# Two recurrent layers in fp32: the second layer's xn transposed in 32x32 blocks by VectorE and carried to its partitions by DMAs, the first layer's additions made by accumulating DMAs

## The chip, the cores and the metric

The kernel runs on one core of one Trainium2 chip. The metric is the device time of one launch in microseconds (us), taken as the median of several runs. Engines are named as in the profile: PE is TensorE's matrix products, PEld its weight loads, DVE is VectorE, ACT is ScalarE, POOL is GpSimd, SP is SyncE, whose queue issues most of the DMAs. The core has an on-chip memory of 128 partitions (SBUF) and a smaller accumulator memory (PSUM), into which TensorE writes its products in banks of 128x512 fp32.

## The reference

The input x is (4, 512, 256) in fp32: four batches of 512 rows. Two layers follow each other. Cut to what matters:

```python
x = L0_attn_x                                   # (B, S, D) = (4, 512, 256)
xn = _layernorm(x)                              # no gain, no offset
s = xn + rmsnorm(((xn @ W_in.T) * g) @ W_out.T) * norm_w     # first layer's mixer, g = sum(C_r*B_r - C_i*B_i)
x = x + s * silu(ffn0(xn))
xn = _layernorm(x)
h = layernorm(xn) * gamma + beta                # second layer's mixer: causal attention
s = softmax(mask(q(h) @ k(h).T / 16)) @ v(h) @ o_proj + xn
x = x + s * silu(ffn1(xn))
# ffn(xn) = fwht(silu(xn @ W1.T) * (xn @ W3.T)) @ W2.T, hidden width 1024, fwht a fixed 1024x1024 matrix
```

The state of the first layer's recurrence starts at zero and is used for one step, so that its mixer is linear up to the RMS norm, as written above. Each layer thus needs xn twice: by rows (for the residual and the gate) and transposed (features on the partitions), because TensorE contracts over partitions.

## The kernel before, in words

**Numbers.** TensorE multiplies fp32 by parts: each operand is held as a rounded part `hi` and the rest `lo`, and a product is three products, hi·hi, hi·lo and lo·hi (`mm3`). `split` (L59 to L62) makes the parts: ScalarE copies `hi` (L61), VectorE subtracts to get `lo` (L62). All matrix products and transposes are issued by one helper line, L70; in the profile they are told apart by their tiles.

**First layer.** It goes by batches 0 to 3. `ffn` (L470) runs over eight chunks of the hidden width. A chunk has two up products (tiles `f_1gu` and so on, twelve matmuls of 128x512 into the banks `gu`, of which there are three), the silu (ScalarE, L531), the product of both halves (VectorE, L533, tile `h`), its split, and the down products of the chunk before (`dn`, 12 matmuls of 128x256). Each chunk has two slots in which other work is issued (`Beside`): the batch's own mixer, the gate of the batch before, the layernorm of the next batch (`norm`, L434) and the preparation of weights. `mixer` (L721) multiplies xn by one folded matrix into the tile `osb`, norms it (L734 to L738: `ssr` holds the mean squares, POOL takes the power -1/2, four VectorE operations scale `osb`), and adds it into the rows of xn (L741, one operation of 128x1024). `gate` (L697) takes the silu of the down products (ScalarE, L704), multiplies it by xn (VectorE, L710, two operations of 128x512, tile `g`) and adds it into x (L712, two of 128x512). A scheduler that works on a simulated timeline orders the instructions of each engine in this layer; `after(...)` adds an order that it has to keep.

**Second layer.** From the last gate of the first layer on, TensorE's order is written out by hand (`line["fixed"] = True`, L1083, `in_line`). For each batch `ffn_s` (L568) goes through four quarters of the hidden width. A quarter has seven products of blocks (`A11`·`B11`, `S1`·`T1`, ... , each six matmuls of 128x256) and between them eight places; `places[q][n]` lists the steps that are issued at place n of quarter q. An integer in the list is a group of six down products of the quarter before (`behind`). The weights of a quarter, 14 blocks of 128x256 in two tiles `sw`, come by two DMAs of 896 KB (L351) from the DRAM tiles `s` that the first layer has written (`prep_s`). The other steps are the attention of the same batch (`v`, `sc`, `soft`, `pt`, `pv`), the gate of the batch before (`gate_half`, then `later_gates`), and what the next batch needs:

- `norm(1, b)` has three steps: the layernorm (L264 to L280: statistics, POOL's power L278, four VectorE operations L280 that write the rows of xn); the second norm's scale `mr` (`second_norm`, L256); and a transpose of `mr`, which goes through a DRAM tile and comes back as `mrb`, one value per row on all partitions.
- `Attention.xt_half(k)` (L751) has TensorE transpose half k of xn into a PSUM bank, four transposes of 128x128.
- `Attention.xt` (L755) makes from the two banks the blocks that the next batch's products need: the sums t1 to t4, the splits `tb11` and `tb2x`, and the products with `mrb` (`fs`); ScalarE copies one half bank (`b12`) first, since an operation of VectorE here takes one operand from PSUM.
- `scaled` (L776) makes the attention's input `xg` from `fs`, `split_sums` (L785) splits t1 to t4, and `tq` (L788) is the first product that reads `xg`.

For batch 0 these steps stand in the slots of the last batch of the first layer. For batches 1 to 3 the transposes and `xt` stand in places 1 and 2 of quarter 2 of the batch before. Pools of tiles set when memory comes free: `t4` has 10 buffers of 4 KB a partition, `t2` 6, `hid` 14, `xn` 3; PSUM has three banks `ms` for transposes and attention, three `gu` and two `dn`. SyncE's queue issues in program order the loads of x and weights, the writes of `s`, the loads of `sw`, `rows` and `mrb` (L452, L454) and the stores of the output (L1054, L1070); an issue whose data is not ready holds up those behind it.

Of the kernel before, what the change touches and what calls it, by code (L numbers as in the profile page):

```python
# [11 lines left out]
F32 = mybir.dt.float32  # L12
# [9 lines left out]
P = 128  # L22
D = 256
# [12 lines left out]
def kernel(ctx: ExitStack, tc: tile.TileContext, a: dict, out: bass.AP):  # L36
# [263 lines left out]
    ALLS = slice(0, S)  # L300
    ALLD = slice(0, D)

    xns, xTs, mrs = {}, {}, {}

    def xt_pair(name):

# [70 lines left out]
    def norm_first():  # L377
# [53 lines left out]
        first["norm"] = hi_, lo_  # L431
        yield

    def norm(layer, b):  # L434
        xn = act.tile([P, NT, D], F32, tag="xn", name=f"xn{layer}_{b}", bufs=3)
        xns[layer, b] = xn
        with after(first["gate"] if b > 1 - layer else None):
            first["scaled"], mv, r = layernorm(f"ln{layer}_{b}", xs[b], xn)
        yield
        if layer:  # L440


            mr = act.tile([P, NT], F32, tag="mr", name=f"mr{b}", bufs=2)
            second_norm(mr, mv, r)
            yield
            o = psum(f"mrp{b}", [NT, P], **DN[b == 0])
            transpose(o, mr, ident)
            rows = act.tile([NT, P], F32, tag="rows", name=f"rows{b}", bufs=1)
            with after(first["table"] if b else None):
                nc.scalar.copy(rows, o)  # L450
            there = dram.tile([NT, P], F32, tag="rows", name=f"there{b}")
            nc.sync.dma_start(there, rows)  # L452
            mrb = t4(f"mrb{b}", [P, S])
            nc.sync.dma_start(  # L454
                mrb, there.rearrange("t p -> (t p)").unsqueeze(0).to_broadcast([P, S])
            )
            mrs[b] = mrb
            yield
            return
        hi, lo = xTs[0, b] = xt_pair(f"xt0_{b}")  # L460
        for k in range(2):
            o = transpose_half(f"xt0_{b}", xn, k)
            first["xt"] = line["last"]
            split(o, hi[:, k, :], lo[:, k, :])
            yield

    def after(ins):
        return tc.issue_after(ins.ins) if ins else nullcontext()
# [99 lines left out]
    def ffn_s(name, b, pairs, w2, beside, before, last=None):  # L568
# [45 lines left out]
        for q in range(NH // 2):  # L614
# [29 lines left out]
            z = bank(f"{q}z")  # L644
            product(z, S1, T1, begin=True)
            h1, v, h0 = halves(f"h1_{q}"), halves(f"v{q}"), halves(f"h0_{q}")
            copy(h1, z)
            place(2)
            product(gate_, S2, T2)
            copied = copy(v, gate_)  # L650
            for what in left:
                with after(copied), after(first["table"]):
                    first["table"] = what()[0]
            left = []
            place(3)
            product(z, S4, B22, end=True)
# [6 lines left out]
            place(5)  # L663
            product(lin, A12, B21, end=True)
            silu(h1, h1)
            nc.vector.tensor_tensor(h1, h1, v, ALU.mult)
            hs = [(halves(f"hh{i}_{q}", F32R), halves(f"hl{i}_{q}", F32R)) for i in range(2)]
            split(h1, *hs[0])
            place(6)
# [11 lines left out]

            left.append(run(split, h0, *hs[1]))
            if q:
                left.pop()()
            place(7)
            behind = units(q, hs)
        if last is None:
# [6 lines left out]
            if (q, c) == (3, 1):  # L694
                last(t, outs[t])

    def gate(name, dn, s, x, store=None, halves=range(2)):  # L697

        rest = []
        for i in halves:  # L700
            ts_ = slice(2 * i, 2 * i + 2)
            g = t2(f"{name}g{i}", [P, 2, D])
            with after(first["table"]):
                first["table"] = nc.scalar.activation(g, dn[i], AF.Silu)  # L704
            rest.append((g, ts_))

        def add():
            for i, (g, ts_) in zip(halves, rest):
                with after(first.get("moments")):
                    nc.vector.tensor_tensor(g, g, s[:, ts_, :], ALU.mult)  # L710
                with after(first.get("h1") if i else None):
                    nc.vector.tensor_tensor(x[:, ts_, :], x[:, ts_, :], g, ALU.add)  # L712
                if store is not None:
                    store(i, ts_)

        return add

    def gate_all(*args):
        gate(*args)()

    def mixer(b):  # L721

# [14 lines left out]
        for t in range(NT):  # L737
            nc.vector.scalar_tensor_tensor(  # L738
                osb[:, t, :], osb[:, t, :], r[:, t : t + 1], nwb, ALU.mult, ALU.mult
            )  # L740
        nc.vector.tensor_tensor(xn, xn, osb, ALU.add)  # L741
        yield

    class Attention:
# [1 line left out]


        def __init__(self, b):
            self.b, self.halves = b, []

        def xt_half(self, k):  # L751
            self.xn = xns[1, self.b]
            self.halves.append(transpose_half(f"xt1_{self.b}", self.xn, k))

        def xt(self):  # L755
            b, mrb = self.b, mrs[self.b]
            xTs[1, b], (tb11, tb2x, tt) = t_blocks(b)
            self.xg = t4(f"xgh{b}", [P, 2, S], F32R), t4(f"xgl{b}", [P, 2, S], F32R)
            b1, b2 = self.halves
            early, late = slice(0, D), slice(D, S)  # L760
            sums = t4(f"tsum{b}", [P, 4, D])
            t1, t2_, t3, t4_ = (sums[:, i, :] for i in range(4))
            b12 = t2(f"b12_{b}", [P, D])
            nc.scalar.copy(b12, b1[:, early])
            nc.vector.tensor_tensor(t1, b12, b1[:, late], ALU.subtract)
            split(b1[:, late], *tb11)
            nc.vector.tensor_tensor(t3, b2[:, early], b12, ALU.subtract)
            fs = [t2(f"xf{b}_{k}", [P, S]) for k in range(2)]
            nc.vector.tensor_tensor(fs[0], b1, mrb, ALU.mult)
            nc.vector.tensor_tensor(t2_, b2[:, early], t1, ALU.subtract)  # L770
            nc.vector.tensor_tensor(t4_, b2[:, late], t2_, ALU.subtract)
            split(b2.rearrange("p (h n) -> p h n", h=2), *tb2x)
            nc.vector.tensor_tensor(fs[1], b2, mrb, ALU.mult)
            self.fs, self.sums = fs, (sums, *tt)

        def scaled(self):  # L776
# [6 lines left out]
                split(f2, *(z[:, k, :] for z in self.xg))  # L783

        def split_sums(self):  # L785
            split(*self.sums)

        def tq(self, j):  # L788
            b = self.b
            if j == 0:  # L790
                self.tqs = t4(f"tqh{b}", [P, 2, S], F32R), t4(f"tql{b}", [P, 2, S], F32R)
            o = psum(f"tq{b}_{j}", [P, S])
            mm3(o, k_pairs(first["wqk"], sl(j), self.xg, ALLS), late=self.b > 0)
            split(o, self.tqs[0][:, j, :], self.tqs[1][:, j, :])

        def v(self, i, j):
            b = self.b
# [118 lines left out]
    def run(f, *args):  # L916
        return lambda: f(*args)

    def call(f, *args):
        f(*args)  # L920
        yield


# [84 lines left out]
    for b in range(B):  # L1008
# [3 lines left out]
            next(prep)  # L1012
            tasks.append((prep, 12))
        if b:
            tasks.append((call(gate_all, f"g0_{b - 1}", dn, xns[0, b - 1], xs[b - 1]), 1))
        tasks.append((mixer(b), MIXER))
        if b + 1 < B:
            if b:
# [17 lines left out]
        if b == 3:  # L1036
            atts = [Attention(0)]
            at = atts[0]
            parts = run(at.xt_half, 0), run(at.xt_half, 1), at.xt, at.scaled, at.split_sums
            tasks += [(call(f), 1) for f in parts]  # L1040
            norms = {1: norm(1, 1)}
            tasks.append((prep_s(3), 4))
# [43 lines left out]
    for b in range(B):  # L1086
# [15 lines left out]
        if not final:  # L1102
            if b == 0:
# [9 lines left out]
                    [1, later_gates[0]], [pts[1], later_gates[1]], [2], [pv[0], pv[1], 3],  # L1113
                ],
                [
                    [pts[2]], [run(c.xt_half, 0)], [0, run(c.xt_half, 1), c.xt], [pv[2]],
                    [1, c.scaled], [pv[3]], [2, c.split_sums], [3],
                ],
                [[tq[0]], [tq[1]], [0], [v_[0]], [1], [v_[1]], [2], [3]],
            ]  # L1120
            if b + 2 < B:
                norms[b + 2] = norm(1, b + 2)
                places[3][7].append(run(next, norms[b + 2]))
            behind, dn = ffn_s(f"f1_{b}", b, pairs(b), w2_1, places, behind)
        else:
            later = [[(q, c, (2, 3)) for c in range(2)] for q in range(2)]
# [74 lines left out]
```

## Time and profile before

| | |
|---|---|
| Median of three runs | 358.20 us (357.91 to 358.28) |
| The profiled execution's own time | 358.58 us |
| Its span, first to last instruction | 356.8 us |
| Granted TensorE clock, mean | 0.999 |
| Busy: PE, PEld, DVE, ACT, POOL | 351.1, 327.8, 277.5, 197.9, 20.7 us |
| Bytes moved by DMA | 51.19 MB, 143 GB/s in the mean |

| Stage (us from the span's start) | PE busy | DVE busy | ACT busy |
|---|---|---|---|
| first layer, batches 0 to 3 (34 to 172) | 138.0 of 138 | 109.2 | 68.5 |
| second layer, batch 0 (172 to 218) | 46.00 of 46.00 | 35.98 | 28.62 |
| batch 1 (218 to 264.6) | 46.60 of 46.60 | 37.32 | 28.86 |
| batch 2 (264.6 to 310.8) | 46.20 of 46.20 | 36.17 | 28.63 |
| batch 3 (310.8 to 356.8) | 41.73 of 46.00 | 29.73 | 22.98 |

The profile is of one execution. Its span is the time from the first to the last instruction on the core; the execution's own time has 1.8 us more around it. Busy times are sums over the instructions of an engine, and matmuls overlap, so that a PE shown as busy need not be at its peak. A line of the view of groups gives a source line, engine, operation and tiles, the number of instructions, the busy time and the mean of one; a line of a timeline or of the chain gives the start, the length, engine, line and tiles.

### The profile page before, as it was taken

The page shows a single profiled execution, that of the slowest core. Times are in us where ns is not written, and L with a number is a line of the kernel's source. Part 1 is how long each engine was busy: PE and PEld are TensorE (multiplying, and loading weights), DVE is VectorE, ACT ScalarE, POOL GpSimd, SP SyncE. Part 2 cuts the span into 40 slices and gives each one's busy share as a digit, 9 for nine tenths or more (in the row PEclk, how much of TensorE's full clock was granted, in tenths as well). Part 3 has the DMA queues.
Part 4 walks back from the last instruction along what each step waited for, and adds up shares of the span by engine and source line. Part 5 has one row for each costly group of instructions (what it writes and reads, how often), then busy time and mean ns, then how long its engine had stood idle before and what let it go on. Part 6 is the DMA issues. An engine that isn't in the chain of part 4 may idle for free.

```text
span 356.8 us, 6246 instructions
## 1 busy us (share of the span) xinstructions
PE 351.1 (98%) x2477; PEld 327.8 (92%) x2477; DVE 277.5 (78%) x562; ACT 197.9 (55%) x374; POOL 20.7 (6%) x22
## 2 busy tenths in 40 slices
PE   8999999999999999999999999999999999999995
PEld 6878998888988898988999999999999999999994
DVE  5899749998579928997787957989579796577646
ACT  3766166266463434854467745587555676556443
POOL 2000110300020300100200001100011000000000
PEclk9999999999999999999999999999999999999999
DMA  7925000301044425567056145562554645445401
GB/s 225 354 85 214 2 1 2 111 6 61 0 159 158 158 70 183 205 233 283 2 208 234 28 180 208 201 218 85 206 183 155 209 165 206 149 148 187 196 2 59
DMA packets 16252, 51.19 MB, mean 143 GB/s; under 512 B 1616, under 2 KB 7904, under 8 KB 16224
## 3 DMA queue, kind: packets, MB, share of 16 engines
q1 hardware_dynamic: 15936, 50.54, 39.7%
q8 instruction: 19, 0.31, 0.4%
q10 hardware_dynamic: 288, 0.26, 0.2%
q14 instruction: 9, 0.07, 0.1%
HBM read 41.36 MB, written 9.45 MB: 142 GB/s over the span
## 4 chain that ended last, share of the span: by engine, by line
PE 98%; DVE 1%; ACT 0%; issue 0%
PE f_0dn L70 6%; PE f_1dn L70 6%; PE f_2dn L70 6%; PE f_0gu L70 6%; PE f_1gu L70 6%; PE f_2gu L70 6%; PE f_3gu L70 6%; PE f_3dn L70 6%; PE sc L70 4%; PE pv L70 4%; PE o L70 3%; PE v L70 3%; PE tq L70 3%; PE warm L70 2%; PE w2ps L70 1%; PE pt L70 1%
## 5 line engine op out<-in xcount | busy, mean ns | idle before, releaser
L70 PE MATMUL f_3gu<-xt,w 128*128 128x512 f32 x96 | 25.1, 395 | 0.0
L70 PE MATMUL f_2gu<-xt,w 128*128 128x512 f32 x96 | 24.8, 395 | 0.0
L70 PE MATMUL f_1gu<-xt,w 128*128 128x512 f32 x96 | 24.8, 395 | 0.0
L70 PE MATMUL f_0gu<-xt,w 128*128 128x512 f32 (+1 forms) x108 | 24.3, 378 | 0.0
L70 PEld LDWEIGHTS f_0gu<-xt,w 128*128 128x128 f32 x108 | 18.4, 188 | 4.5 <-issue 1.0
L70 PEld LDWEIGHTS f_1gu<-xt,w 128*128 128x128 f32 x96 | 17.0, 188 | 3.1
L70 PEld LDWEIGHTS f_2gu<-xt,w 128*128 128x128 f32 x96 | 17.0, 188 | 3.0
L70 PEld LDWEIGHTS f_3gu<-xt,w 128*128 128x128 f32 x96 | 17.0, 188 | 2.9
L61 ACT CAST f_2hh<-f_2h 128x512 fp32r<-128x512 f32 x16 | 10.0, 623 | 16.4 <-DVE f_2h L533 12.4
L70 PE MATMUL f_3dn<-w2l,f_3hh 128*128 128x256 f32 x64 | 17.7, 281 | 0.0
L70 PE MATMUL f_3dn<-w2h,f_3hh 128*128 128x256 f32 x64 | 17.7, 281 | 0.0
L70 PE MATMUL f_1dn<-w2l,f_1hh 128*128 128x256 f32 x64 | 17.7, 281 | 0.0
L70 PE MATMUL f_2dn<-w2h,f_2hh 128*128 128x256 f32 x64 | 17.7, 282 | 0.0
L70 PE MATMUL f_1dn<-w2h,f_1hh 128*128 128x256 f32 x64 | 17.6, 281 | 0.0
L70 PE MATMUL f_2dn<-w2l,f_2hh 128*128 128x256 f32 x64 | 17.6, 281 | 0.0
L70 PE MATMUL f_3dn<-w2h,f_3hl 128*128 128x256 f32 x64 | 17.2, 284 | 0.0
L70 PE MATMUL f_1dn<-w2h,f_1hl 128*128 128x256 f32 x64 | 17.0, 281 | 0.0
L70 PE MATMUL f_2dn<-w2h,f_2hl 128*128 128x256 f32 x64 | 16.7, 281 | 0.0
L61 ACT CAST f_3hh<-f_3h 128x512 fp32r<-128x512 f32 (+1 forms) x17 | 10.1, 596 | 11.6 <-DVE f_3h L533 7.4
L61 ACT CAST f_1hh<-f_1h 128x512 fp32r<-128x512 f32 x16 | 9.9, 622 | 10.6 <-DVE f_1h L533 6.6
L62 DVE TENSOR_TENSOR f_3hl<-f_3h,f_3hh 128x512 fp32r<-128x512 f32 (+1 forms) x17 | 11.0, 654 | 4.4 <-ACT f_3hh L61 4.3
L62 DVE TENSOR_TENSOR f_2hl<-f_2h,f_2hh 128x512 fp32r<-128x512 f32 x16 | 11.0, 685 | 4.4 <-ACT f_2hh L61 4.3
(479 smaller groups left out, 1135.2 us busy)
## 6 DMA issues: line engine op xcount, KB each, us to landing
sw<-s SPq DMA_DIRECT2D x32, 896.0 KB, 5.4
s<-sp SPq DMA_DIRECT2D x8, 512.0 KB, 3.3
s<-sp SPq DMA_DIRECT2D x8, 384.0 KB, 2.5
w2raw<-in_w SPq DMA_DIRECT2D x4, 512.0 KB, 5.1
sraw<-in_w SPq DMA_DIRECT2D x4, 512.0 KB, 3.0
w13raw<-in_w SPq DMA_DIRECT2D x3, 512.0 KB, 7.2
x<-in_x SPq DMA_DIRECT2D x3, 512.0 KB, 3.2
out<-x SPq DMA_DIRECT2D x6, 256.0 KB, 2.2
```

Of the source, the lines that this page charges most:

```text
L61: h = nc.scalar.copy(hi, src)
L62: return h, engine.tensor_tensor(lo, src, hi.bitcast(F32), ALU.subtract)
L70: ins = call(*args, **kwargs)
```

## The change

1. **Transposes of the second layer's xn.** The new function `flip` replaces `xt_half`. VectorE transposes the four row tiles of xn in blocks of 32x32 within 32 partitions (one `nc.vector.transpose` of 128x256 each) into a `t4` tile. A DMA on SyncE's queue writes that tile to DRAM (512 KB), and four more (128 KB each) read it back into the same tile, each so that the blocks come to the partitions where the whole transpose wants them. `flip` is issued in the second step of `norm(1, b)`. `xt` then reads the two halves from SBUF in place of PSUM, through strided views (`cut` gives the other operands the same shape); ScalarE's copy `b12` is no longer there. The 32 transposes of 128x128 on TensorE are gone.
2. **Order in the second layer.** Place 1 of quarter 2 now holds only a down group, place 2 holds `xt`; the first step of `norm(1, b + 2)` moves from place 7 to place 2 of quarter 3. `after` pins are added: `xt` behind `copied` and `rounded`, the splits of the sums behind `mult`, the later norms behind `tql`, `flip` behind `rounded`, and the second of the gate's additions behind `low`.
3. **Additions of the first layer.** The mixer's `xn += osb` (L741, all four batches) and the gate's `x += g` (L712, batches 0 to 2, two each) are DMAs from SBUF to SBUF that POOL issues with `accum_op=ALU.add`. The gate of batch 3 keeps VectorE's additions.

```diff
@@ -300,7 +300,7 @@
     ALLS = slice(0, S)
     ALLD = slice(0, D)
 
-    xns, xTs, mrs = {}, {}, {}
+    xns, xTs, mrs, flips = {}, {}, {}, {}
 
     def xt_pair(name):
 
@@ -431,13 +431,37 @@
         first["norm"] = hi_, lo_
         yield
 
+    def flip(name, xn):
+
+
+
+        here = t4(f"{name}flip", [P, 4, D])
+        for t in range(NT):
+            nc.vector.transpose(
+                here.rearrange("p a (t k j) -> p t a k j", t=NT, k=2)[:, t],
+                xn[:, t, :].rearrange("p (k a j) -> p a k j", k=2, j=32),
+            )
+        there = dram.tile([4, P, D], F32, tag="flip", name=f"{name}there")
+        nc.sync.dma_start(there.rearrange("a p n -> p a n"), here)
+        for q in range(4):
+            nc.sync.dma_start(here[:, q, :], there[:, 32 * q : 32 * (q + 1), :])
+        there = here.rearrange("p q (t k j) -> p k t q j", t=NT, k=2)
+        return [there[:, k] for k in range(2)]
+
+    def cut(z):
+        return z.rearrange("p (t q j) -> p t q j", q=4, j=32)
+
     def norm(layer, b):
         xn = act.tile([P, NT, D], F32, tag="xn", name=f"xn{layer}_{b}", bufs=3)
         xns[layer, b] = xn
-        with after(first["gate"] if b > 1 - layer else None):
-            first["scaled"], mv, r = layernorm(f"ln{layer}_{b}", xs[b], xn)
+        with after(first.get("tql") or (first["gate"] if b > 1 - layer else None)):
+            scaled, mv, r = layernorm(f"ln{layer}_{b}", xs[b], xn)
+        if "tql" not in first:
+            first["scaled"] = scaled
         yield
         if layer:
+            with after(first.get("rounded")):
+                flips[b] = flip(f"xt1_{b}", xn)
 
 
             mr = act.tile([P, NT], F32, tag="mr", name=f"mr{b}", bufs=2)
@@ -644,13 +668,13 @@
             z = bank(f"{q}z")
             product(z, S1, T1, begin=True)
             h1, v, h0 = halves(f"h1_{q}"), halves(f"v{q}"), halves(f"h0_{q}")
-            copy(h1, z)
+            first["copied"] = copy(h1, z)
             place(2)
             product(gate_, S2, T2)
             copied = copy(v, gate_)
             for what in left:
                 with after(copied), after(first["table"]):
-                    first["table"] = what()[0]
+                    first["table"], first["low"] = what()
             left = []
             place(3)
             product(z, S4, B22, end=True)
@@ -663,7 +687,7 @@
             place(5)
             product(lin, A12, B21, end=True)
             silu(h1, h1)
-            nc.vector.tensor_tensor(h1, h1, v, ALU.mult)
+            first["mult"] = nc.vector.tensor_tensor(h1, h1, v, ALU.mult)
             hs = [(halves(f"hh{i}_{q}", F32R), halves(f"hl{i}_{q}", F32R)) for i in range(2)]
             split(h1, *hs[0])
             place(6)
@@ -681,7 +705,7 @@
 
             left.append(run(split, h0, *hs[1]))
             if q:
-                left.pop()()
+                first["rounded"] = left.pop()()[1]
             place(7)
             behind = units(q, hs)
         if last is None:
@@ -694,7 +718,7 @@
             if (q, c) == (3, 1):
                 last(t, outs[t])
 
-    def gate(name, dn, s, x, store=None, halves=range(2)):
+    def gate(name, dn, s, x, store=None, halves=range(2), by_dma=False):
 
         rest = []
         for i in halves:
@@ -708,15 +732,18 @@
             for i, (g, ts_) in zip(halves, rest):
                 with after(first.get("moments")):
                     nc.vector.tensor_tensor(g, g, s[:, ts_, :], ALU.mult)
-                with after(first.get("h1") if i else None):
+                if by_dma:
+                    nc.gpsimd.dma_start(x[:, ts_, :], g, accum_op=ALU.add)
+                    continue
+                with after(first.get("h1") if i else None), after(first.get("low") if i else None):
                     nc.vector.tensor_tensor(x[:, ts_, :], x[:, ts_, :], g, ALU.add)
                 if store is not None:
                     store(i, ts_)
 
         return add
 
-    def gate_all(*args):
-        gate(*args)()
+    def gate_all(*args, **kwargs):
+        gate(*args, **kwargs)()
 
     def mixer(b):
 
@@ -738,7 +765,7 @@
             nc.vector.scalar_tensor_tensor(
                 osb[:, t, :], osb[:, t, :], r[:, t : t + 1], nwb, ALU.mult, ALU.mult
             )
-        nc.vector.tensor_tensor(xn, xn, osb, ALU.add)
+        nc.gpsimd.dma_start(xn, osb, accum_op=ALU.add)
         yield
 
     class Attention:
@@ -746,31 +773,31 @@
 
 
         def __init__(self, b):
-            self.b, self.halves = b, []
-
-        def xt_half(self, k):
-            self.xn = xns[1, self.b]
-            self.halves.append(transpose_half(f"xt1_{self.b}", self.xn, k))
-
-        def xt(self):
-            b, mrb = self.b, mrs[self.b]
+            self.b = b
+
+        def xt(self, late=False):
+            pins = ("copied", "rounded") if late else ("gate", "silu")
+            with after(first[pins[0]]), after(first[pins[1]]):
+                self.xt_()
+
+        def xt_(self):
+            b, mrb = self.b, cut(mrs[self.b])
+            self.xn = xns[1, b]
             xTs[1, b], (tb11, tb2x, tt) = t_blocks(b)
             self.xg = t4(f"xgh{b}", [P, 2, S], F32R), t4(f"xgl{b}", [P, 2, S], F32R)
-            b1, b2 = self.halves
-            early, late = slice(0, D), slice(D, S)
+            b1, b2 = flips[b]
+            early, late = slice(0, 2), slice(2, 4)
             sums = t4(f"tsum{b}", [P, 4, D])
-            t1, t2_, t3, t4_ = (sums[:, i, :] for i in range(4))
-            b12 = t2(f"b12_{b}", [P, D])
-            nc.scalar.copy(b12, b1[:, early])
-            nc.vector.tensor_tensor(t1, b12, b1[:, late], ALU.subtract)
-            split(b1[:, late], *tb11)
-            nc.vector.tensor_tensor(t3, b2[:, early], b12, ALU.subtract)
+            t1, t2_, t3, t4_ = (cut(sums[:, i, :]) for i in range(4))
+            nc.vector.tensor_tensor(t1, b1[:, early], b1[:, late], ALU.subtract)
+            split(b1[:, late], *(cut(z) for z in tb11))
+            nc.vector.tensor_tensor(t3, b2[:, early], b1[:, early], ALU.subtract)
             fs = [t2(f"xf{b}_{k}", [P, S]) for k in range(2)]
-            nc.vector.tensor_tensor(fs[0], b1, mrb, ALU.mult)
+            nc.vector.tensor_tensor(cut(fs[0]), b1, mrb, ALU.mult)
             nc.vector.tensor_tensor(t2_, b2[:, early], t1, ALU.subtract)
             nc.vector.tensor_tensor(t4_, b2[:, late], t2_, ALU.subtract)
-            split(b2.rearrange("p (h n) -> p h n", h=2), *tb2x)
-            nc.vector.tensor_tensor(fs[1], b2, mrb, ALU.mult)
+            split(b2, *(z.rearrange("p h (t q j) -> p (h t) q j", q=4, j=32) for z in tb2x))
+            nc.vector.tensor_tensor(cut(fs[1]), b2, mrb, ALU.mult)
             self.fs, self.sums = fs, (sums, *tt)
 
         def scaled(self):
@@ -783,7 +810,8 @@
                 split(f2, *(z[:, k, :] for z in self.xg))
 
         def split_sums(self):
-            split(*self.sums)
+            with after(first.get("mult")), after(first["table"]):
+                split(*self.sums)
 
         def tq(self, j):
             b = self.b
@@ -791,7 +819,9 @@
                 self.tqs = t4(f"tqh{b}", [P, 2, S], F32R), t4(f"tql{b}", [P, 2, S], F32R)
             o = psum(f"tq{b}_{j}", [P, S])
             mm3(o, k_pairs(first["wqk"], sl(j), self.xg, ALLS), late=self.b > 0)
-            split(o, self.tqs[0][:, j, :], self.tqs[1][:, j, :])
+            lo = split(o, self.tqs[0][:, j, :], self.tqs[1][:, j, :])[1]
+            if b:
+                first["tql"] = lo
 
         def v(self, i, j):
             b = self.b
@@ -916,8 +946,8 @@
     def run(f, *args):
         return lambda: f(*args)
 
-    def call(f, *args):
-        f(*args)
+    def call(f, *args, **kwargs):
+        f(*args, **kwargs)
         yield
 
 
@@ -1012,7 +1042,7 @@
             next(prep)
             tasks.append((prep, 12))
         if b:
-            tasks.append((call(gate_all, f"g0_{b - 1}", dn, xns[0, b - 1], xs[b - 1]), 1))
+            tasks.append((call(gate_all, f"g0_{b - 1}", dn, xns[0, b - 1], xs[b - 1], by_dma=True), 1))
         tasks.append((mixer(b), MIXER))
         if b + 1 < B:
             if b:
@@ -1036,7 +1066,7 @@
         if b == 3:
             atts = [Attention(0)]
             at = atts[0]
-            parts = run(at.xt_half, 0), run(at.xt_half, 1), at.xt, at.scaled, at.split_sums
+            parts = at.xt, at.scaled, at.split_sums
             tasks += [(call(f), 1) for f in parts]
             norms = {1: norm(1, 1)}
             tasks.append((prep_s(3), 4))
@@ -1113,14 +1143,14 @@
                     [1, later_gates[0]], [pts[1], later_gates[1]], [2], [pv[0], pv[1], 3],
                 ],
                 [
-                    [pts[2]], [run(c.xt_half, 0)], [0, run(c.xt_half, 1), c.xt], [pv[2]],
+                    [pts[2]], [0], [run(c.xt, True)], [pv[2]],
                     [1, c.scaled], [pv[3]], [2, c.split_sums], [3],
                 ],
                 [[tq[0]], [tq[1]], [0], [v_[0]], [1], [v_[1]], [2], [3]],
             ]
             if b + 2 < B:
                 norms[b + 2] = norm(1, b + 2)
-                places[3][7].append(run(next, norms[b + 2]))
+                places[3][2].append(run(next, norms[b + 2]))
             behind, dn = ffn_s(f"f1_{b}", b, pairs(b), w2_1, places, behind)
         else:
             later = [[(q, c, (2, 3)) for c in range(2)] for q in range(2)]
```

## The prediction

> **What bounds the kernel now.** I read the page's busy times and its chain first, then the list of waits of TensorE, then the chain around the transposes that the change removes, and last the timelines of the engines at the two places where new waits come in.
>
> ```profile
> PE 351.1 (98%) x2477; PEld 327.8 (92%) x2477; DVE 277.5 (78%) x562; ACT 197.9 (55%) x374; POOL 20.7 (6%) x22
> PE 98%; DVE 1%; ACT 0%; issue 0%
> PE warm L70 <- DVE zr L935: 1.4, 1, 1.4
> ```
>
> The first two lines say that TensorE is busy in 98% of the span and that the chain that ended last lies on it for 98%. The third is the whole list of TensorE's waits: one, of 1.4 us, at the start. In the stretches 34 to 310 us TensorE shows no idle time at all, at a granted clock of 1.00. So time is won only by taking work from TensorE, and lost only where a new wait reaches it. VectorE's 78% matters only as slack.
>
> **Removed from TensorE.** Each batch's second-layer xn loses eight 128x128 transposes. The chain shows what they take (start, length, engine, tile, count):
>
> ```profile
> 193.08 0.44 PE pt L70 x4
> 193.52 0.44 PE xt_1tp L70 x4
> 193.96 0.72 PE f_0gu2z L70 x6
> 194.68 0.71 PE f_0dn L70 x6
> 195.39 0.44 PE xt_1tp L70 x4
> ```
>
> Two groups of four at 0.44 us: 0.88 a batch. Batches 2 and 3 show the same 0.44 (at 239.8 and 241.6 for batch 2). Batch 0's eight lie in the first layer in groups of 3, 4 and 1; the chain has 0.33 and 0.44, the single one I put at 0.11. So 4 x 0.88 = 3.5 us, all of it on TensorE's path. The recorded length of one is 0.27 us, but they overlap; the chain is the price. The Trainium skill (TensorE: Matmul & The Clock Gate, Part 4: PE-mode transpose) gives about 275 ns for a transpose in a kernel's context; by that the gain would be 32 x 0.275 = 8.8 us, an estimate from that page. The chain's 0.11 us decides.
>
> **Moved: the order in quarter 2.** With the transposes gone, a group of six down products (`behind` 0) goes ahead of z's product. It needs the low half of h1, on VectorE at 192.33 to 193.0; TensorE asks for it at about 193.6. That holds by 0.6 us. The xt step reads SBUF instead of PSUM; its eight VectorE operations keep their sizes (0.33 us a 128x256, 0.60 a 128x512), and ScalarE's copy of b12 (0.38) goes. The xg halves move ahead of the sums on VectorE, so they are ready some 3 us earlier than their 203.9 to 204.6, and tq (204.5, then 203.6) is not late.
>
> **Added to VectorE: four block transposes a batch.** No row shows one. The nearest are the four 128x256 operations of the norm (L280, 1.38 together); the dearest of about this size is the reduction of 128x512 (0.6). So 1.3 to 2.4 us a batch; I take 1.4, the same elements in and out. They lie where VectorE has room: for batch 1 in front of L659, which waits 1.15 us for TensorE at 176.9; for batches 2 and 3 at the batch boundary, where the norm's 1.38 and its 1.1 wait for POOL stood before and are now moved into quarter 3, into the 2.3 us that L659 waits there. What is late next is L662 behind L280: by 0.5 us at most, and A22's product after it has about that much to spare. I put 0; without that cover it is up to 0.5 a batch, 1.5 us.
>
> **Added to SyncE's queue: one 512 KB write and four 128 KB reads a batch.** Write: 3.3 us (s<-sp, 512 KB). Reads: four issues of 0.33, then 1.7 (out<-x, 128 KB) to 3.1 (mrb). In sum 6.3 to 7.7, and up to 7 more if they stand behind weight loads in the rings. The consumers come 19 us later (batch 1: about 176.5 to 195.6), 22 later (batch 2: about 219 to 241.75), 20 later for batch 0. The queue waits for the write to land, and behind it stand loads of weights:
>
> ```profile
> 203.06 23.32 SPq L351 DMA_DIRECT2D sw<-s  x6
> 226.44 0.43 SPq L1054 DMA_DIRECT2D out<-x  x1
> sw<-s SPq DMA_DIRECT2D x32, 896.0 KB, 5.4
> s<-sp SPq DMA_DIRECT2D x8, 512.0 KB, 3.3
> ```
>
> For batches 2 and 3 write and reads fall into the gap before the load at 226, which waits for TensorE anyway. For batch 1 the reads stand between the two halves of quarter 2's weights: the second half goes out at about 182.5 instead of 181.3, lands by 188 to 190 and is needed at 191.3 (192.2 less 0.9). Zero, with 1.5 us to spare; without that, up to 1 us once.
>
> **First layer: additions by accumulating DMAs.** Four mixer sums (L741, 1.22 us each) and six gate sums (L712, 0.64 each) leave VectorE: 8.7 us that bound nothing. Five of the seven groups have over 15 us until their reader: xn of batches 1 to 3 is read by the next gate 20 us on, x by the next layer's norm over 20 us on. POOL's small powers stand behind these issues but are asked for later. One does not: the mixer's sum of batch 0, whose reader, the gate's product L710, is next in VectorE's queue, and in front of f_1h.
>
> ```profile
> 49.79 1.66 DVE L738 SCALAR_TENSOR_TENSOR osb<-osb,ssr,nwb 128x256 f32<-128x256 f32 x4
> 51.97 1.22 DVE L741 TENSOR_TENSOR xn<-xn,osb 128x1024 f32<-128x1024 f32 x1
> 53.29 1.29 DVE L710 TENSOR_TENSOR g_0g<-g_0g,xn 128x512 f32<-128x512 f32 x2
> 56.58 0.69 DVE L533 TENSOR_TENSOR f_1h<-f_1h,f_1gu 128x512 f32<-128x512 f32 x1 [0.80 <-ACT f_1h L531]
> 57.89 3.42 PE L70 MATMUL f_1gu<-xt,w 128*128 128x512 f32 x14
> 61.15 0.28 PE L70 MATMUL f_1dn<-w2h,f_1hh 128*128 128x256 f32 x1
> ```
>
> osb is done at 51.45; the DMA can go then. f_1h starts at 56.58 now. Its product frees the PSUM bank that chunk 2's first product takes: the ninth of the fourteen matmuls, 57.89 + 8 x 0.233 = 59.75. The down product at 61.15 needs ScalarE's f_1hh after it (57.73 to 58.35): 2.8 us. So f_1h may come 2.5 us later at no cost, at 59.1; with L710's 1.25 before it the DMA must have landed by 57.8, that is 6.3 us after it may start. Every us beyond is a us of TensorE; the wait counts once, as later chunks are shifted alike.
>
> No row shows an accumulating DMA, nor one that POOL issues. From below: a plain 512 KB, 3.2 us (x<-in_x), and an issue of 0.3: 3.5. From above: w13raw, 512 KB in the crowded start, 7.2, or win with 8.7, and a slow POOL operation of 1.9 (L278 at 65 us): 10.6. Between: the sum reads source and destination, so some 1 MB is read; nearest is the 896 KB load at 5.4 us, and one POOL operation at 1.0: 6.4. I take that, because the rings are idle at 51 to 60 us (1 to 2 GB/s in these slices). Stall 6.4 - 6.3 = 0.1; bounds 0 and 4.3.
>
> The Trainium skill (SBUF — State Buffer, "SBUF: two separate sides") speaks against this edit: while VectorE runs an operation in a 2-port mode, POOL cannot write descriptors for its DMAs, and a DMA of 620 ns took 3100. By that page it would add about 2.5 us, but it also says that tensor_tensor has no such mode. Between 51.4 and 53 us VectorE's queue holds only the second half of the split of xt, a TENSOR_TENSOR of 0.68 us, so by the trace nothing is added.
>
> **Sum.** Against the profiled execution, 358.58 us (span 356.8 and 1.8 around it): 358.58 - 3.5 + 0.1 = 355.2. That execution lies 0.38 above the median of 358.20; so 354.8 in the median. About 0.2% (0.7 us) is what a measurement of this kernel can tell from no change.
>
> **Rivals.** *The accumulating DMA is somewhat late:* landing 7 to 9 us after its start stalls TensorE by 0.7 to 2.7 and gives 355.4 to 357.4. For: it is the first such DMA of the program, and a read and a write of SBUF each way. Against: idle rings. *It is very late, and the kernel is slower:* from 3.5 + 0.7 us of stall on, that is from 10.5 us of landing time at this one place, time is over 358.9; at 13 us it is 361.5. For: no row bounds the descriptors that POOL writes, and the queue behind the wait is VectorE's whole first-layer work. Against: it needs more than win's 8.7 in the full rings plus POOL's slowest operation. Landing at 9 to 10.5 gives no change. *Second-layer waits:* the norm in quarter 3, the transposes at the boundary and batch 1's weights cost up to 0.5 a batch and 1 once: 1 to 2 us, 356 to 357. For: margins of 0.4 to 0.6 us stand by my sums. Against: VectorE has 36 of 46 us a batch. *Vector time pays:* that the 8.7 us taken off VectorE give a gain of their own; against it, TensorE waits for nothing after 1.4 us. It would end below 354.2; hardly any chance.
>
> **How the numbers follow.** Forecast (stall under 0.7): 0.55. Somewhat late: 0.13. Second-layer waits: 0.09. No change: 0.06. Slower: 0.16. Below: 0.01. Faster is 0.55 + 0.13 + 0.09 + 0.01 = 0.78. The range starts at 354.2 (3.5 and half a us of reordered groups) and reaches to the upper bound of the DMA, 354.7 + 4.3 = 359.0; what lies above is about 0.14.
>
> **What would show it.** Right: 32 fewer transposes, no wait of TensorE around 59 us, a span of about 353.4, xt's first VectorE operation never waiting for a DMA. Wrong: TensorE idle near 59 us with VectorE's L734 ended by a DMA (the landing time is then read off), or TensorE waiting for VectorE's L686 at the end of quarter 3 or for sw in batch 0, or block transposes over 0.6 us each.

## The result, and the profile after

The changed kernel takes 360.19 us (median of six runs, 359.48 to 361.98) against 358.13 for the kernel before: a ratio of 1.0063, interval 1.0047 to 1.0079. It is slower by 2.1 us where a gain of 3.4 was forecast. The profiled execution took 360.99 us with a span of 358.8; it lies 0.8 above its median.

The page's busy line and the head of its chain:

```profile
PE 349.7 (97%) x2445; PEld 324.5 (90%) x2445; DVE 274.8 (77%) x568; ACT 196.7 (55%) x370; POOL 28.0 (8%) x32
PE 86%; DMA 10%; DVE 2%; ACT 1%; issue 0%; SPq 0%; DVEq 0%; ACTq 0%
```

The 32 transposes are gone (2477 to 2445 products), but a chain that was TensorE to 98% now runs through DMAs for 10% of the span. The list of TensorE's waits has five entries where it had one:

```profile
PE warm L70 <- DVE zr L965: 1.5, 1, 1.5
PE f_3dn L70 <- ACT f_3hh L61: 1.4, 1, 1.4
PE f_0gu2g L70 <- DMA sw<-s: 0.9, 1, 0.9
PE f_2gu2g L70 <- DMA sw<-s: 0.2, 1, 0.2
PE f_0gu2g L70 <- DVE f_0h L686: 0.2, 1, 0.2
```

The list leaves out short waits, because a matmul's end is modelled and covers them. Read from the starts in TensorE's timeline (time from one start to the next, beyond what that tile usually takes), the stalls of this execution are:

| At (us) | Stall | The product waits for |
|---|---|---|
| 139 | 1.64 | ScalarE's f_3hh, behind a load of raw weights |
| 190, 237, 283 | 0.36 each | the low half of h0, behind L686 on VectorE |
| 194 | 1.19 | second half of quarter 2's weights, batch 0 |
| 204 | 0.42 | L686 of quarter 2, batch 0, late because mrb was late |
| 287 | 0.50 | second half of quarter 2's weights, batch 2 |
| 296 | 0.28 | as at 204, batch 2 |

Their sum is 5.1 us. Less the 3.5 us of the transposes that is +1.6, and TensorE's last product indeed ends at 354.19 in place of 352.53. The other 0.75 of the 2.41 between the two profiled executions lie behind the last product and outside the span.

**Where the stalls come from.** All but the three of 0.36 lead to SyncE's queue. SyncE's timeline of the kernel before around 130 us, and then that of the changed kernel:

```profile
128.84 0.32 SPq L452 DMA_DIRECT2D there<-rows  x1
130.02 0.34 SPq L454 DMA_DIRECT2D mrb<-there  x1
130.41 0.42 SPq L326 DMA_DIRECT2D sraw<-in_w  x1
```

```profile
122.03 0.37 SPq L445 DMA_DIRECT2D xt_0there<-xt_0flip  x1
125.58 2.40 SPq L447 DMA_DIRECT2D xt_0flip<-xt_0there  x4
130.31 0.28 SPq L476 DMA_DIRECT2D there<-rows  x1
134.21 0.36 SPq L478 DMA_DIRECT2D mrb<-there  x1
134.66 0.38 SPq L326 DMA_DIRECT2D sraw<-in_w  x1
```

mrb's issue waits until the 2 KB of rows have landed, and the load of raw weights (sraw) stands behind it. Before, rows took 1.2 us; now it takes 3.9, and sraw goes out at 134.66 in place of 130.41. The chain around this place shows who pays:

```profile
130.31 3.88 DMA there<-rows
...
134.66 5.08 DMA sraw<-in_w
...
140.55 0.62 ACT f_3hh L61
...
141.22 0.74 PE f_3dn L70 x4
```

ScalarE's copy of sraw stands in its queue ahead of f_3hh, for which the down product waits; f_3h itself was ready at 135.48:

```profile
139.81 0.83 ACT L61 CAST sp<-sraw 128x768 fp32r<-128x768 f32 x1 [5.17 <-DMA sraw<-in_w]
```

Why rows is slow shows in the table of stretches. Its last two columns are the mean busy share of the 16 DMA engines and GB/s; the first line lies in the time of the flip's write, the second in that of its four reads, the last of which was issued by 127.98:

```profile
123.00:125.00 2.00, 2.00 (x10) 1.62 (x10) 1.65 (x4) 0.84 (x2) 0.25 (x1) 1.00 0.76 253
128.00:133.00 5.00, 5.00 (x36) 4.58 (x35) 0.69 (x1) 1.30 (x3) 0.00 (x0) 1.00 0.27 92
```

While only the reads are under way, 0.27 of the engines are busy: 4.3 of 16. The packets say the same: about 90 of 1 KB in each us at 46 to 49 ns are 4.2 engines. At these four engines a flip's 512 packets take about 6 us, and rows waits there. The trace's records of single packets agree: from 128 to 133 us never fewer than 4 and never more than 6 are under way, the last packet of the reads ends at 133.43, and rows' four packets run from 133.30 to 133.47. In batch 0 of the second layer the weights wait too:

```profile
177.51 0.37 SPq L445 DMA_DIRECT2D xt_1there<-xt_1flip  x1
180.71 0.32 SPq L351 DMA_DIRECT2D sw<-s  x1
181.13 2.44 SPq L447 DMA_DIRECT2D xt_1flip<-xt_1there  x4
183.66 1.70 SPq L351 DMA_DIRECT2D sw<-s  x1
185.46 0.29 SPq L476 DMA_DIRECT2D there<-rows  x1
194.70 0.35 SPq L478 DMA_DIRECT2D mrb<-there  x1
```

rows now takes 9.2 us to land (3.0 before). The stretches show how the weights end:

```profile
186.00:191.00 5.00, 4.90 (x42) 4.70 (x41) 3.56 (x8) 4.33 (x9) 0.00 (x0) 1.00 0.86 208
191.00:194.00 3.00, 2.58 (x22) 2.38 (x21) 2.78 (x6) 1.75 (x4) 0.00 (x0) 1.00 0.25 96
```

From 191 to 194 us the engines' share is 0.25, and four or five packets are under way in 95% of the time: four engines work off what is left of the reads and of the weights, after the others have finished theirs. TensorE's product stops at 193.6 until 194.50, and mrb comes so late that VectorE stands still for 2.69 us in front of L796, with the sums and L686 behind it:

```profile
194.50 0.74 PE L70 MATMUL f_0gu2g<-tb,sw 128*128 128x256 f32 x4 [0.92 <-DMA sw<-s]
199.82 0.69 DVE L796 TENSOR_TENSOR xf<-xt_1flip,mrb 128x512 f32<-128x512 f32 x1 [2.69 <-DMA mrb<-there]
```

**The 0.36 three times** is VectorE's order in quarter 1. The low half of h0 (L62) used to go ahead of the addition that makes h1; now it stands behind it, and that addition waits for TensorE. Before, and then in the changed kernel:

```profile
187.63 0.69 DVE L62 TENSOR_TENSOR f_0hl<-f_0h,f_0hh 128x512 fp32r<-128x512 f32 x1
188.24 0.68 DVE L662 TENSOR_TENSOR f_0h<-f_0gu1g,f_0h 128x512 f32<-128x512 f32 x1
```

```profile
188.78 0.69 DVE L686 TENSOR_TENSOR f_0h<-f_0gu1g,f_0h 128x512 f32<-128x512 f32 x1 [0.47 <-PE f_0gu1g L70]
189.39 0.68 DVE L62 TENSOR_TENSOR f_0hl<-f_0h,f_0hh 128x512 fp32r<-128x512 f32 x1
```

The down product that reads the low half starts at 190.12, when L62 ends, 0.37 after its predecessor in place of 0.12, and the next one 0.22 after it.

### The profile page after: what moved, and what is told of

Its sections match the earlier page's. It is cut to its first block, busy times and chain, and to the rows that moved or that the text cites. A ratio compares the mean times of both kernels' runs of the same rounds, so it can differ in the third digit from the quotient of the medians.

```text
span 358.8 us, 6269 instructions
## 1 busy us (share of the span) xinstructions
PE 349.7 (97%) x2445; PEld 324.5 (90%) x2445; DVE 274.8 (77%) x568; ACT 196.7 (55%) x370; POOL 28.0 (8%) x32
## 4 chain that ended last, share of the span: by engine, by line
PE 86%; DMA 10%; DVE 2%; ACT 1%; issue 0%; SPq 0%; DVEq 0%; ACTq 0%
PE f_1dn L70 6%; PE f_0gu L70 6%; PE f_2gu L70 6%; PE f_1gu L70 6%; PE f_3dn L70 6%; PE f_0dn L70 5%; PE f_3gu L70 5%; PE f_2dn L70 5%; DMA there<-rows 4%; PE sc L70 4%; DMA sw<-s 3%; PE v L70 3%; PE tq L70 3%; PE pv L70 3%; PE o L70 2%; PE warm L70 2%
## 5 line engine op out<-in xcount | busy, mean ns | idle before, releaser
L62 DVE TENSOR_TENSOR f_3hl<-f_3h,f_3hh 128x512 fp32r<-128x512 f32 (+1 forms) x17 | 11.1, 656 | 4.3 <-ACT f_3hh L61 4.1
L70 PEld LDWEIGHTS f_3dn<-w2h,f_3hh 128*128 128x128 f32 x64 | 12.1, 188 | 2.2 <-ACT f_3hh L61 1.8
```

The costliest lines, as they stand in the source:

```text
L62: return h, engine.tensor_tensor(lo, src, hi.bitcast(F32), ALU.subtract)
L70: ins = call(*args, **kwargs)
```

## The experiments

The theories: **A**, the four reads of a flip run on four DMA engines, and what follows them in the queue waits there, plus the order of the low half; **B**, it is the bytes and the places in the queue as such; **C**, it is the accumulating DMAs.

**Reads spread over all engines** (e1). The bytes and the number of DMAs are the same; the outer order of the reads is 32 in place of 4, and the write has pieces of 4 KB:

```diff
-        there = dram.tile([4, P, D], F32, tag="flip", name=f"{name}there")
-        nc.sync.dma_start(there.rearrange("a p n -> p a n"), here)
-        for q in range(4):
-            nc.sync.dma_start(here[:, q, :], there[:, 32 * q : 32 * (q + 1), :])
+        there = dram.tile([P, 4, D], F32, tag="flip", name=f"{name}there")
+        nc.sync.dma_start(there, here)
+        back = there.rearrange("(q r) a n -> a r q n", q=4)
+        for i in range(4):
+            nc.sync.dma_start(here[32 * i : 32 * (i + 1), :, :], back[i])
```

> The changed kernel, with another layout of the DRAM tile: the write keeps whole partitions (128 rows of 4 KB), and each of the four reads brings 32 partitions with four pieces of 1 KB, where it brought 128 partitions with one piece each in an outer order of four. Same bytes, same number of DMAs, same order. Theory A, the four reads of a flip run on four of the sixteen DMA engines (in the changed kernel's trace 88 to 94 packets of 1 KB in each us at 46 to 49 ns, a share of 0.27, for 6 us), and what follows in SyncE's queue (the 2 KB write of rows, mrb, the next weights) waits for these four: the reads take under 3 us, rows lands within 4 us in place of 9 to 10, and TensorE's stalls at 139 (1.5 us), 194 (1.1), 204 (0.3), 287 and 296 (0.5 together) go: 360.2 less 2.5 to 3.5, 356.7 to 357.7 us. Theory B, the added bytes and the places in the queue cost the time however the reads are spread: within 0.5 us of 360.2. Theory C, the accumulating DMAs of the first layer cost it: 359.5 to 360.2.

Measured: 356.15 us, a ratio of 0.9947 to the kernel before (0.9932 to 0.9962): 4.0 us faster than the changed kernel, 0.5 below the range of A, and faster than before. Its runs lie within 0.12 us of each other, where those of the changed kernel spread over 2.5. Here are the stretch of its reads, SyncE's timeline and the whole list of TensorE's waits:

```profile
126.00:128.50 2.50, 2.50 (x16) 2.19 (x16) 1.02 (x2) 0.62 (x1) 0.00 (x0) 1.00 0.76 208
```

```profile
129.92 0.30 SPq L477 DMA_DIRECT2D there<-rows  x1
131.09 0.35 SPq L479 DMA_DIRECT2D mrb<-there  x1
131.54 0.38 SPq L326 DMA_DIRECT2D sraw<-in_w  x1
```

```profile
PE warm L70 <- DVE zr L966: 1.5, 1, 1.5
```

The reads take 2.5 us at a share of 0.76, rows lands in 1.2 us again (5.6 in batch 0 of the second layer, over the 4 us expected but early enough), and all stalls behind DMAs are gone. Only the three gaps of 0.36 are left. B and C cannot explain this: neither bytes nor accumulating DMAs were changed. But the write and the layout in DRAM were changed too, so this run alone does not single out the reads.

**The write alone** (e9): the same write, but the reads keep their outer order of four (`here[:, q, :]` from `there[32 * q : 32 * (q + 1)].rearrange("r a n -> a r n")`).

> The changed kernel with only the write of the wide variant (128 rows of 4 KB); the four reads keep their outer order of four, 128 partitions with one piece of 1 KB each. Theory A (the reads' outer order puts them on four engines): 360.2 us within 1.0, and again about 90 packets of 1 KB in each us at a share of 0.27 after the write. Rival (the gain of the wide variant came from the write's larger pieces): 356.2 us.

Measured: 358.93 us (358.08 to 362.35), ratio 1.0031 (1.0007 to 1.0055), still slower than before. The reads again hold four engines: rows takes 4.1 us at 130 (1.2 with the reads spread) and 8.9 at 185, and the stall of the first layer stays (1.6 in the list).

```profile
129.84 0.28 SPq L478 DMA_DIRECT2D there<-rows  x1
133.91 0.35 SPq L480 DMA_DIRECT2D mrb<-there  x1
```

Between e9 and e1 only the reads' order differs, so 2.8 of the 4.0 us are that order. The other 1.3, more than I had allowed, came with the write and its layout, in which the 1 KB pieces of a read lie 4 KB apart in DRAM; in this trace the weights of batch 0 are late by 0.5 in place of 1.2 and those of batch 2 not at all. Whether the write's larger pieces or the layout does that was not separated, and the runs of this kernel spread over 4 us.

**Sixteen reads** (e10): layout and write as in the changed kernel, each read cut into four of 32 partitions.

> The changed kernel with its layout and its write; each of the four reads is cut into four of 32 partitions, so that no read has an outer order of four. Sixteen issues at 0.45 to 0.6 us take 7 to 10 us of SyncE's queue in place of 2.4. Theory A: the reads use all engines, and rows lands within 4 us of its issue; what the longer issue costs is bounded by the slack of the weights behind it: 356.2 to 358.5 us. Rival (the layout matters, not the order of the reads): 360 us or, with the longer queue, more.

Measured: 360.5 us, ratio 1.0086 (1.0058 to 1.0115): the range of A was wrong, and the time is the one that the rival named. Its reason is not borne out by the trace: layout and write are the changed kernel's, yet the first-layer stall is gone and rows lands in 1.3 us there (4.2 to 6.0 in the second layer). But sixteen issues hold SyncE for 9 us, so that the second half of the weights goes out at 188.16, and TensorE waits for weights in batches 0, 1 and 2 (1.5, 1.0 and 1.1 us):

```profile
178.99 9.07 SPq L448 DMA_DIRECT2D xt_1flip<-xt_1there  x16
188.16 0.37 SPq L351 DMA_DIRECT2D sw<-s  x1
```

Issue time in the one queue is thus a second price beside the engines. The second half went out 7.1 us later than in e1 (181.01, no stall) and TensorE lost 1.8, so the slack behind it is, as an estimate, about 5 us. While these reads are issued the share of the engines is as low as with the narrow ones:

```profile
126.00:132.00 6.00, 6.00 (x44) 5.58 (x43) 1.38 (x2) 1.40 (x3) 0.00 (x0) 1.00 0.26 70
```

Here it is low because the queue gives out only 32 KB in each 0.46 us; the packets under way swing between 0 and 15. A low share alone does not tell a narrow pattern from a slow issue. In the changed kernel it stays at 0.27 for 5 us after the last read has been issued, with four packets or more at every moment.

**rows and mrb issued by POOL** (e7): `nc.gpsimd.dma_start` for these two, the narrow reads kept.

> The changed kernel with its narrow reads, but the write of rows and the read of mrb issued by POOL in place of SyncE, so that the queue with the weights no longer waits for the 2 KB of rows to land. Theory A in two parts: the load of raw weights at 134.7 goes out some 4 us earlier and the stall at 139 us (1.5) goes, mrb may still be late since its packets need the same four engines; the stalls at the weights of batches 0 and 2 (1.2 and 0.5) stay: 360.2 less 1.5 to 2.2, 358.0 to 358.7 us. If the whole loss were SyncE's wait for rows: 356 us. If it is nothing but the weights on the four engines: 360 us.

Measured: 358.15 us, ratio 0.9999 (0.9988 to 1.0010), inside the range of A. sraw now goes out right behind the reads, and the stall at 139 us is gone; the waits for weights stay:

```profile
125.37 2.39 SPq L447 DMA_DIRECT2D xt_0flip<-xt_0there  x4
127.87 0.44 SPq L326 DMA_DIRECT2D sraw<-in_w  x1
```

```profile
PE f_0gu2g L70 <- DMA sw<-s: 0.8, 1, 0.8
PE f_2gu2g L70 <- DMA sw<-s: 0.4, 1, 0.4
```

The stalls of mrb's lateness at 204 and 296 us are gone too. (The list has one more entry, 0.5 us for the first layer's xn at 6 us, long before anything that this edit touches.) About 2.0 us of the loss thus goes with rows and mrb standing in SyncE's queue.

**Accumulating DMAs alone** (e3): the kernel before with the first layer's additions as DMAs.

> The kernel before, with the first layer's additions (all four of the mixer, six of the gate) made by accumulating DMAs, and TensorE's transposes kept. Theory A: the accumulating DMAs cost nothing where nothing is queued late: 358.1 us within 0.4. Theory C (their traffic delays the loads and the weights of the first layer): 359 to 360 us, with a stall of TensorE between 100 and 166 us. As predicted before the run, the first one lands about 5 us after its issue and TensorE does not wait near 59 us.

Measured: 358.44 us, ratio 1.0008 (0.9998 to 1.0017): no difference that is clear. TensorE waits for nothing after the start. At the upper end of the interval the accumulating DMAs cost 0.6 us: C is out as the cause of the loss.

**Additions back on VectorE** (e4), in the changed kernel.

> The changed kernel with the first layer's additions back on VectorE; transposes by VectorE and DMAs kept as they are. Theory A (reads on four engines): the second layer's stalls stay (1.2 at the weights of batch 0, 0.36 three times), the stall at 139 us in the first layer shrinks only as far as the load of raw weights (5.1 us to landing beside an accumulating DMA, 3.0 without) comes earlier: 358.7 to 360.0 us. Theory C (accumulating DMAs are the loss): 355.5 to 357 us.

Measured: 361.55 us, ratio 1.0099 (1.0081 to 1.0116), above the range of A and far from C. The stalls at 139 (1.9 us in the list) and at the weights of batch 0 (1.1) stay, and two are new: 0.8 for f_3h at 158 us and 0.4 for the weights of batch 1. The load of raw weights takes 4.57 us here without an accumulating DMA beside it, 5.08 in the changed kernel, so those DMAs were not what made it late. The wait at 158 follows the next such load in the chain: it goes out at 151.69, and the work on it by ScalarE and VectorE (156.27 to 158.34) stands before f_3h. That it is VectorE's time, which the DMAs had saved, that is missed there is my reading and was not tested alone.

**The low half first** (e2): `with after(first.get("low") if q == 1 else None):` around L686.

> The changed kernel, with the addition that makes h1 in the second quarter (VectorE) pinned behind the subtraction that makes the low half of the quarter before. In the changed kernel the low half had fallen behind that addition, which waits for TensorE, and a down product waits 0.36 us for the low half in each of batches 0 to 2. Theory A (part of the loss is this order): 0.36 x 3 = 1.1 less, 359.1 us, and no gap of TensorE at 190, 237 and 283 us. Rival: the products after it wait for weights and mrb anyway, so that the time is taken back by the next wait in batches 0 and 2: 0.4 less, 359.8 us. If the waits are not by this order: 360.2.

Measured: 361.02 us, ratio 1.0079 (1.0063 to 1.0096). No gain: the three gaps are gone, but the stalls behind DMAs in the profiled execution are larger (2.0 at 139 and 1.3 at the weights in its list, 1.4 and 0.9 in the changed kernel's). That execution had a mean clock of 0.992; the other three, at 0.997 to 1.000, are as slow (360.69 to 361.04). By itself this run settles nothing.

**Both** (e5): reads spread and the low half first.

> Both edits at once: the reads spread as in the wide variant, and the low half pinned ahead of the second quarter's addition. In the wide variant's trace TensorE waits for nothing after the start but three gaps of 0.36 us (at 188, 233 and 279 us), each a down product that wants the low half. Theory A (what is left of the loss is this order, and the pin alone did not show because later waits for DMAs took its gain back): 356.15 less 1.1 = 355.1 us, no gap left, 3.0 us under the kernel before. Rival (the pin itself costs, as its lone run at 361.0 may be read): 356.2 or more.

Measured: 355.08 us, ratio 0.9914 (0.9898 to 0.9931): 1.07 under e1, as three times 0.36 should give, and 3.0 under the kernel before. TensorE's only wait is the first. (The run e6 was a second profile of this kernel: 355.54 us.) In the pair e1 and e5 the order of the low half is shown to cost 1.1 us. That it was hidden in e2 by what the DMAs took fits e2's larger stalls; why they grew is not shown.

**The best version with the additions on VectorE** (e8).

> Reads spread and low half first, as in the best version, with the first layer's additions back on VectorE. Theory: with the reads spread no chain of DMAs is late in the first layer, and the 8.7 us of VectorE's time that the additions take bound nothing: 355.1 us within 0.5. Rival: VectorE's slack in the last batch of the first layer was needed for the block transposes and the sums of the weights (with narrow reads the additions on VectorE cost 1.3 us, 361.5 against 360.2): 356 to 357 us.

Measured: 354.96 us, ratio 0.9909 (0.9892 to 0.9925), the same as e5. Once the reads are spread, the accumulating DMAs are worth nothing that can be measured. e5 and e8 beat both kernels.

## Why the prediction was wrong, step by step

Forecast and result lie 5.4 us apart (354.8 and 360.19). Of these, 4.0 went with the write and reads of the flip (e1) and 1.1 with the order of the low half (e5); e5's 355.08 is what was forecast, within 0.3.

**Removed transposes: right.** 32 at 0.11 us, 3.5 us. With all stalls gone, e5 is 3.0 us under the kernel before by the medians of one session (355.08 and 358.05). The two profiled executions differ by 3.5 (355.06 and 358.58), but that of before is one of its slowest. So the term is right within half a us.

**First accumulating DMA, the main risk of the forecast: right in kind, a little high in size.** It was put at 6.4 us from osb's end with 6.3 free. osb was done at 51.32; the issue began at 51.93 and the data was there at 56.73: 5.4 us. The first 0.6 of it the issue stood until VectorE's split of xt (L62) was done; the prediction had put that operation at nothing, and why POOL waited for it is open. f_1h came at 57.95, inside the 59.1, and TensorE did not wait. VectorE's and POOL's timelines of the changed kernel:

```profile
51.93 1.05 POOL L768 DMA_DIRECT2D xn<-osb  x1 [2.43 <-DVE xt L62]
56.73 1.29 DVE L734 TENSOR_TENSOR g_0g<-g_0g,xn 128x512 f32<-128x512 f32 x2 [4.81 <-DMA xn<-osb]
57.95 0.68 DVE L557 TENSOR_TENSOR f_1h<-f_1h,f_1gu 128x512 f32<-128x512 f32 x1
```

**Block transposes on VectorE: right.** Taken at 1.4 us a batch; measured 1.34 (176.06 to 177.40 for batch 1).

```profile
L440 DVE STREAM_TRANSPOSE xt_1flip<-xn x4: 405/406/442, 176.1 to 177.1; 128x256 f32<-128x256 f32 x4
```

**SyncE's queue: the step that failed.** The flip itself was early enough, as forecast: xt's first operation (L792) never waits for it. What failed is the zero for what stands behind the reads, in three things. First, the price: the reads were put at 1.7 to 3.1 us behind 1.3 of issue, 3.0 to 4.4, by rows of DMAs whose patterns are cut otherwise (out<-x, mrb). They took 7.9 in the first layer (125.58 to 133.43), since they ran on four engines. I looked at what the reads move, not at how their pattern is cut. Second, the weights: for batch 1 I let the second half go out at 182.5 and land by 188 to 190, with 1.5 us to spare. It went out at 183.66, in a trace that was 2.0 us behind by then (the flip's write is issued at 177.51, in e1 at 175.50), so not too late; but it took 10.8 us to land in place of 5.5 to 7.5, and TensorE stood until 194.50. Third, the list: the rows, mrb and raw weights of the first layer's last batch, and rows and mrb of every later batch, were not on it, although SyncE's timeline of before shows them there. That is where 2.0 us went by e7.

The Trainium skill (DMA: Bandwidth & Descriptors, "Rules for kernel authors", the row on using all 16 engines) says that a pattern whose outermost dimension has c < 16 entries keeps the whole DMA on at most c engines. The section on why a DMA increments its semaphore by 16 adds that SyncE's DMAs take the lowest-numbered ones. The trace agrees with the first: 0.27 of 16 engines. By the second the 4x128 write of rows would share just the engines that the reads hold; no run here shows engine numbers, but rows' 9.2 us fit. This rule speaks against the change as written, and the prediction did not weigh it.

**The order of the second layer: half right.** The low half of h1 in quarter 2, with its margin of 0.6, and the moved norm cost nothing: in e5 TensorE has no gap there. What came in was one quarter earlier, the low half of h0 behind L686, which the prediction did not name and so put at nothing: 0.36 a batch, 1.1 in sum. Its rival of second-layer waits has 1 to 2 us in sum, but from the norm, the transposes and batch 1's weights; of these only the weights came, and that the 1.1 falls in its span is chance.

**VectorE's 8.7 us pay nothing: right**, by e3 and e8. Beside narrow reads (e4) they may count: 1.4 us by the medians, in runs that overlap. Of its seven groups of additions the prediction names five with time and one without; the seventh held nothing up either, since in e3 TensorE waits for none.

**What would show it.** The prediction named TensorE waiting for sw in batch 0 as a sign that it is wrong, and that came. Its rival of a slower kernel, at a chance of 0.16, had the sign right for a wrong reason: the late DMA was not the accumulating one in front of VectorE's queue but four plain reads in front of SyncE's.

## What to carry to other kernels

Price a DMA by its pattern, not only by its bytes: look in a trace for a row with the same outer order, and if there is none, bound its time by the share of engines that it could be held to (here 7.9 us where 3.0 to 4.4 were allowed). Then write down everything that stands behind it in its queue until the next idle stretch, the 2 KB transfers above all, because a small transfer that someone waits for can be as late as the large ones ahead of it (here 3.9 and 9.2 us for 2 KB, in place of 1.2 and 3.0). And when a step moves work between engines, compare the order of every engine in the quarters next to it too: three gaps of 0.36 us came from the order alone, and their gain showed only after the larger stalls were out of the way.

## What the runs showed of the hardware

Four reads of 128 KB with an outer order of four moved 92 GB/s at a share of 0.27; the same bytes with an outer order of 32 moved 208 GB/s at 0.76. A 2 KB write took 1.2 us to land behind the spread reads in the first layer and 3.9 behind the narrow ones; with weights in the queue as well, in batch 0 of the second layer, 5.6 and 9.2. A 512 KB accumulating DMA from SBUF to SBUF landed 4.8 us after its issue began where little else was moving, and 5.5 us in the median of four. Sixteen reads of 32 KB held SyncE's queue for 7.3 to 9.1 us, four of 128 KB with the same bytes for 2.2 to 2.4.
